# Signs, right combinations and row maxima of a two-layer graph kernel: a written order, another engine, and transposes

## The chip, the cores and the metric

The kernel runs on one core of a Trainium2 chip. The metric is the device time of one execution in microseconds; the time of a version is the median of its runs. An instruction belongs to an engine: TensorE (PE in the profile, its weight loads PEld), VectorE (DVE), ScalarE (ACT), GpSimd (POOL) or SyncE (SP, which here only issues transfers). Each engine works off its own queue in order and waits on semaphores for the others.

## The reference

`x` is 4096 x 512, `adj` 4096 x 4096 with non-negative entries, and all is float32. Two layers, each followed by a residual and a layer norm:

```python
# layer 0
xw  = maximum(sign(x), 0) @ sign(w0).T
x1  = layernorm(x + relu(adj @ xw))
# layer 1
node_att = softmax(x1 @ node_w, axis=0)
h   = x1 @ edge_w
e   = where(adj > 0, h @ h.T, NEG_BIG)
out = layernorm(x1 + (adj * (node_att * softmax(e, axis=1))) @ (x1 @ w1) + bias)
```

## The kernel before, in words

The 4096 rows are 32 blocks of 128, or 8 groups of 4 blocks (512 rows). The kernel goes through five stages, each bound to what the one before leaves in SBUF or in DRAM.

**Signs** (lines 167 to 256). `whole(g)` makes the four blocks of xw of a group g in two multiplications of 128 rows. Two blocks of signs are packed into one operand, `ba = [a > 0] + 2048 * [b > 0]` (lines 211 and 212, or 186 and 187 for group 0; the intermediate is `over0`). The weights' signs `bw` are made on VectorE in two passes a quarter (lines 204 and 206). The product `pw` is taken apart by a large shift: `us` on ScalarE (line 220), the low block on VectorE (222), the high one on ScalarE (223). In group 0 the four quarters of x and w0 arrive by separate transfers, and TensorE is kept active by multiplications of zeros (`zeros`).

Meanwhile the adjacency product of the first two row blocks (0 and 4, `early`) is accumulated. `halves(g)` loads two pieces `a`, rounds them to `hi` on ScalarE (line 236) and takes the remainder `lo` on VectorE (237); `follow(g)` multiplies both with xw, 16 matmuls a group (246 and 247). `hi`, `lo`, `over0` and `pos` come from one pool with two buffers a tag; `over0` has the tag of `hi`. `x` and w0 go through three buffers of `stream`, `a` through four of `rows`. A scheduler chooses the order on every engine here.

**Aggregation of layer 0** (345 to 384). For the other 30 blocks, `at` is split and multiplied in the same way (363 to 374, 64 matmuls a block); `rest` makes the layer norm and the products with `node_w`, and `transpose_rows` turns x1 into `x1T` with four transposes a block (333). `premask` loads pieces of adj, turns them into masks on VectorE (281) and stores them on GpSimd's queue (282). The order on VectorE and ScalarE is the written one.

**h** (387 to 429). `h.T` is made in four pairs of groups. Each pair is one step of a seven-product scheme: four combinations of the right operand, t1 to t4 (lines 417 to 420), t3 on GpSimd and the others on VectorE, and then `seven` (95 to 144), whose products go to three banks for each half q. A product that accumulates into a bank waits until VectorE or ScalarE has read what stood there. `between_h` is called between products and calls `premask` for three ticks of five. Tiles t1, t2 come from the tag of `hi`, t3, t4 from that of `lo`.

**e and its row maxima** (452 to 763): h @ h.T by blocks, with each block's negated row maximum in `nmax_c`.

**Aggregation of layer 1** (766 to 1420): 16 units `Aggregate(g, r)`, a written plan with due times as shares of a unit. Before the units of a group pair, `panel(A)` (777) spreads the maxima of 512 rows over all partitions: for each of its 4 blocks a multiplication takes the column of maxima, broadcast to 128 columns, as its stationary operand and the identity as the moving one (784). The result goes to `mrow` on ScalarE (795), which `shift` subtracts from e (835). There are eight panels, two before the units start and two ahead of each later group pair; the first pair stands in the stage of e. `Finish` ends rows with a product by w1 (1208) that VectorE adds to x1 (1219).

Of the kernel before, what the change touches and what calls it, by code (L numbers as in the profile page):

```python
# [22 lines left out]
TWO = 2.0**11  # L23
SHIFT = 1.5 * 2.0**34
SPLIT = 6, 4, 3
WARM = 12
# [3 lines left out]
def kernel(  # L30
# [128 lines left out]
    with (  # L159
# [14 lines left out]

        us = wp.tile([P, BG // 2, D], F32, name="us", tag="ends")

        def whole(g):

            xt = stream.tile([P, KD, W], F32, name="xt", tag="stream")
            ba = wp.tile([P, KD, W // 2], F32R, name="ba", tag="quarter", bufs=2)  # L180
            pws = [ps_mm.tile([P, D], F32, name="pw", tag="mm") for j in range(BG // 2)]
            order = [(k, j) for j in range(BG // 2) for k in range(KD)]

            def signs(k, over):
                a, b = xt[:, k, : W // 2], xt[:, k, W // 2 :]
                nc.vector.tensor_scalar(over, b, 0.0, TWO, ALU.is_gt, ALU.mult)
                nc.vector.scalar_tensor_tensor(ba[:, k, :], a, 0.0, over, ALU.is_gt, ALU.add)

            if g == 0:

                pos = sp.tile([P, KD, D], BF16, name="pos", tag="lo")
                over = sp.tile([P, KD, W // 2], F32, name="over0", tag="hi")
                for k in range(KD):
                    nc.sync.dma_start(w0[:, k, :], w0_t[ts(k, P), :])
                    nc.scalar.dma_start(xt[:, k, :], x_t[ts(k, P), ts(g, W)])
                idle = ps_mm.tile([P, D], F32, name="idle", tag="mm")

                def zeros(n):
                    for _ in range(n):
                        nc.tensor.matmul(idle, warm[:, :P], warm, start=True, stop=True)  # L200

                zeros(WARM)
                for k in range(KD):
                    nc.vector.tensor_scalar(pos[:, k, :], w0[:, k, :], 0.0, None, ALU.is_gt)
                    signs(k, over[:, k, :])
                    nc.vector.scalar_tensor_tensor(bw[:, k, :], w0[:, k, :], 0.0, pos[:, k, :], ALU.is_lt, ALU.subtract)
                order = [(k, j) for k in range(KD) for j in range(BG // 2)]
            else:
                nc.sync.dma_start(xt, x_t[:, ts(g, W)].rearrange("(k p) n -> p k n", p=P))
                over = sp.tile([P, KD, W // 2], F32, name="over0", tag="hi")  # L210
                nc.vector.tensor_scalar(over, xt[:, :, W // 2 :], 0.0, TWO, ALU.is_gt, ALU.mult)
                nc.vector.scalar_tensor_tensor(ba, xt[:, :, : W // 2], 0.0, over, ALU.is_gt, ALU.add)
            for k, j in order:
                nc.tensor.matmul(pws[j], ba[:, k, ts(j, P)], bw[:, k, :], start=(k == 0), stop=(k == KD - 1))  # L214
                if g == 0 and j == BG // 2 - 1:
                    zeros(3 if k < KD - 1 else 5)
                if k == KD - 1:

                    u = us[:, j, :]
                    nc.scalar.activation(u, pws[j], AF.Identity, bias=shift[:, 0:1])  # L220
                    b = g * BG + j
                    nc.vector.scalar_tensor_tensor(xw[:, b, :], u, SHIFT, pws[j], ALU.subtract, ALU.subtract)
                    nc.scalar.activation(xw[:, b + BG // 2, :], u, AF.Identity, bias=shift[:, 1:2], scale=-1.0 / TWO)


        early = [0, BG]
        accs = []

        def halves(g):

            hi = sp.tile([P, QC, P], F32R, name="hi", tag="hi")
            lo = sp.tile([P, QC, P], F32R, name="lo", tag="lo")
            for n, b in enumerate(early):
                a = rows.tile([P, BG, P], F32, name="a0", tag="rows")
                nc.sync.dma_start(a, adj_t[b, :, ts(g, BG), :])
                nc.scalar.copy(hi[:, ts(n, BG), :], a)
                nc.vector.tensor_sub(lo[:, ts(n, BG), :], a, hi[:, ts(n, BG), :].bitcast(F32))
            return hi, lo

        def follow(g, hi, lo):  # L240
            if g == 0:
                accs.extend(ps_tr.tile([P, D], F32, name="acc0", tag="tr") for _ in early)
            for n in range(2):
                for c in range(BG):
                    kb = g * BG + c
                    nc.tensor.matmul(accs[n], hi[:, n * BG + c, :], xw[:, kb, :], start=(kb == 0), stop=False)  # L246
                    nc.tensor.matmul(accs[n], lo[:, n * BG + c, :], xw[:, kb, :], start=False, stop=(kb == NB - 1))  # L247

        whole(0)
        parts = halves(0)  # L250
        for g in range(NG):
            if g + 1 < NG:
                whole(g + 1)
            follow(g, *parts)
            if g + 1 < NG:
                parts = halves(g + 1)

        nw_b = wp.tile([P, D], F32, name="nw_b")
        nc.sync.dma_start(nw_b, bass.AP(tensor=node_w.tensor, offset=node_w.offset, ap=[[0, P], [1, D]]))
# [31 lines left out]
        def rest(n, b, xb, acc, before):  # L291

            mv = small.tile([P, 1, nc.vector.BN_AGGR_DIM], F32, name="mv")
            stats = small.tile([P, nc.vector.BN_STATS_DIM], F32, name="stats")
            rstd = small.tile([P, 1], F32, name="rstd")
            scr = wp.tile([P, D], F32, name="scr")
            nc.vector.scalar_tensor_tensor(xb, acc, 0.0, xb, ALU.max, ALU.add)
            nc.vector.bn_stats(stats, xb)
            nc.vector.bn_aggr(mv[:, 0, :], stats)
            yield  # L300
            nc.scalar.activation(rstd, mv[:, :, 1], AF.Sqrt, bias=eps)
            nc.vector.reciprocal(rstd, rstd)
            nc.vector.tensor_scalar(xb, xb, mv[:, 0, 0:1], rstd[:, 0:1], ALU.subtract, ALU.mult)
            nc.vector.tensor_tensor_reduce(
                scr, xb, nw_b, 1.0, 0.0, ALU.mult, ALU.add, accum_out=node_s[:, b : b + 1]
            )
            yield
            nc.vector.tensor_add(scr, xb, bias_b)
# [28 lines left out]
        parts = deque()  # L337
# [65 lines left out]
        for _ in range(4):  # L403
            premask(nc.sync, 0, 3)
        count = [0]

        def between_h(q, n):
            count[0] += q is None
            if q is None and count[0] > 6 and count[0] % 5 % 2 == 0:
                premask(nc.sync, 0, 3)  # L410

        for g in range(HG):
            r11, r12 = (x1T[:, :HK, ts(c, W)] for c in (g, g + HG))
            r21, r22 = (x1T[:, HK:, ts(c, W)] for c in (g, g + HG))
            t1, t2 = (sp.tile([P, HK, W], F32, name="t12", tag="hi") for _ in range(2))
            t3, t4 = (sp.tile([P, HK, W], F32, name="t34", tag="lo") for _ in range(2))
            nc.vector.tensor_sub(t1, r12, r11)
            nc.gpsimd.tensor_sub(t3, r22, r12)
            nc.vector.tensor_sub(t2, r22, t1)
            nc.vector.tensor_sub(t4, r21, t2)  # L420
            right_h = r11, r21, r22, t4, t1, t2, t3
            seven(
                lambda m, q: [left_h[m][:, k, ts(q, P)] for k in range(HK)],
                lambda m: [right_h[m][:, k, :] for k in range(HK)],
                [[hT[:, q + f, ts(c, W)] for f in (0, HK) for c in (g, g + HG)] for q in range(2)],
                between_h,
            )
# [349 lines left out]
    def panel(A):  # L777
# [4 lines left out]
        for i in range(BG):  # L782

            nc.tensor.matmul(
                pt[:, ts(i, P)],
                nm[:, i : i + 1].to_broadcast([P, P]),
                ident,
                start=(i == 0),
                stop=True,
                skip_group_check=i > 0,  # L790
            )
        if A > 1:
# [664 lines left out]
```

## Time and profile before

| | |
|---|---|
| median of 5 runs | 1937.34 us (1936.02 to 1939.8) |
| the profiled execution | 1939.8 us, its span 1937.8 us |
| granted TensorE clock, mean | 0.998 |
| first matmul of the aggregation of layer 0 (line 373) | at 57.13 us |
| first product of h, first product of e | at 507.44 and 605.80 us |
| first product of the aggregation of layer 1 | at 1091.94 us |
| busy of the engines from 507 to 606 us | PE 97.9, DVE 67.6, ACT 12.4, POOL 32.5 us |
| data moved | 508.72 MB, mean 263 GB/s |

A span runs from the first to the last instruction. A row of the timeline has start, duration, engine, line, operation, output and inputs, and at its end, in brackets, how long the engine had been idle and what released it. The ends of matmuls are modelled: one of 512 columns is shown with 0.39 us (fp32r) though the next starts 0.23 us after it, so starts are compared, not durations. Some rows that the steps below use, each as mean duration:

| line | engine | what | us |
|---|---|---|---|
| 204, 206 | DVE | bw, a quarter | 0.42, 0.68 |
| 186, 187 | DVE | over0 and ba of group 0, a quarter | 0.29, 0.42 |
| 211, 212 | DVE | over0 and ba, a whole group | 0.69, 1.23 |
| 220, 223 | ACT | us, high block of xw | 0.69, 0.72 |
| 222 | DVE | low block of xw | 0.69 |
| 236, 237 | ACT, DVE | hi, lo | 0.62, 0.69 |
| 417, 419, 420 | DVE | t1, t2, t4 | 1.22 to 1.23, one 3.27 |
| 418 | POOL | t3 | 2.36 to 3.20 |

Independent neighbours on an engine overlap by some 0.1 us of these.

### The profile page before, as it was taken

Reading aid. Unit: us, or ns where it says so; the run is one execution under the profiler, and the core shown is the slowest. Engines: PE = TensorE matmul, PEld = TensorE weight load, DVE = VectorE, ACT = ScalarE, POOL = GpSimd, SP = SyncE. Lnnn points to the kernel's source line nnn. Section 1 sums busy time; section 2 is a strip of 40 time slices with the busy share of each in tenths; the row PEclk is TensorE's granted clock in tenths of the full one; section 3 lists DMA queues with packets and bytes.
Section 4 is the critical chain, followed back from the end, with each engine's and each line's share of the span. In section 5 each row is a group of like instructions: output and inputs, shape, how many; then the busy total and the mean of one; then the engine's idle time right before and its main releaser. Section 6 shows DMA issues by size and latency. Waiting matters only on the chain.

```text
span 1937.8 us, 20238 instructions
## 1 busy us (share of the span) xinstructions
PE 1919.1 (99%) x6742; PEld 1204.2 (62%) x6742; DVE 1389.7 (72%) x2062; ACT 1022.4 (53%) x1614; POOL 292.2 (15%) x413
## 2 busy tenths in 40 slices
PE   9999999999999999999999999999999999999998
PEld 6888888888644445454556444456666666666655
DVE  7766676676765566567665986687869987798747
ACT  5433333333202567566677666546766576757731
POOL 0122222222341111011111111111111110111100
PEclk9999999999999999999999999999999999999999
DMA  8888888888475478577783998787778777877731
GB/s 308 299 326 309 293 324 306 326 305 291 152 274 214 165 254 318 184 280 252 278 314 105 347 328 290 264 273 257 260 265 291 261 272 260 293 274 262 274 109 44
DMA packets 169527, 508.72 MB, mean 263 GB/s; under 512 B 15696, under 2 KB 41040, under 8 KB 161744
## 3 DMA queue, kind: packets, MB, share of 16 engines
q1 hardware_dynamic: 89472, 226.39, 35.1%
q0 software_dynamic: 64688, 239.10, 32.9%
q10 hardware_dynamic: 15264, 41.95, 5.9%
q8 instruction: 53, 0.87, 0.2%
q14 instruction: 50, 0.41, 0.1%
HBM read 385.74 MB, written 121.63 MB: 262 GB/s over the span
## 4 chain that ended last, share of the span: by engine, by line
PE 88%; issue 4%; DMA 4%; DVE 3%; ACT 1%; POOL 1%; POOLq 0%; DVEq 0%; SPq 0%
PE bank L1081 32%; PE seven L714 15%; PE acc L374 11%; PE acc L373 11%; PE pe L641 6%; PE po L1208 3%; PE seven L101 3%; PE pt L603 3%; DMA slot<-s_d 1%; DMA lent<-s_d 1%; PE pw L214 1%; PE acc L246 1%; PE pt L333 1%; PE acc L247 1%; DMA over<-in_w_dram 1%
## 5 line engine op out<-in xcount | busy, mean ns | idle before, releaser
L1081 PE MATMUL bank<-lent,lop 128*128 128x512 f32 (+1 forms) x1136 | 420.0, 517 | 0.0
L373 PE MATMUL acc<-xw,hi 128*128 128x512 f32 x960 | 376.4, 392 | 0.0
L374 PE MATMUL acc<-xw,lo 128*128 128x512 f32 x960 | 374.2, 390 | 0.0
L1081 PE MATMUL bank<-slot,lop 128*128 128x256 f32 (+1 forms) x1052 | 357.8, 488 | 1.9 <-DVE slot L862 1.9
L1081 PEld LDWEIGHTS bank<-lent,lop 128*128 128x128 f32 x1136 | 215.7, 190 | 173.9 <-issue 158.8
L1081 PEld LDWEIGHTS bank<-slot,lop 128*128 128x128 f32 x1052 | 200.2, 191 | 136.7 <-issue 116.4
L363 ACT CAST hi<-at 128x1024 fp32r<-128x1024 f32 x120 | 126.4, 1054 | 203.4 <-PE acc L373 148.4
L365 DVE TENSOR_TENSOR lo<-at,hi 128x1024 fp32r<-128x1024 f32 x120 | 148.0, 1234 | 84.7 <-ACT hi L363 84.7
L374 PEld LDWEIGHTS acc<-xw,lo 128*128 128x128 f32 x960 | 180.3, 188 | 37.0 <-DVE lo L365 0.3
L373 PEld LDWEIGHTS acc<-xw,hi 128*128 128x128 f32 x960 | 180.3, 188 | 36.7
L1090 ACT COPY over<-bank 128x512 f32<-128x512 f32 x200 | 114.3, 580 | 108.3 <-PE bank L1081 95.3
L641 PE MATMUL pe<-hT 128*128 128x512 f32 (+3 forms) x384 | 132.1, 486 | 0.0
L574 ACT ACTIVATE line<-line,nmax_c 128x512 f32<-128x512 f32 x160 | 114.8, 725 | 22.5 <-DVE nmax_c L565 22.3
L565 DVE CUSTOM_DVE_ANT_0 line<-lent,slot 128x512 f32<-128x512 bf16 x140 | 90.7, 688 | 48.4 <-ACT slot L651 26.7
L835 DVE CUSTOM_DVE_ANT_1 lent<-lent,line 128x2048 f32<-128x2048 f32 x40 | 91.4, 2286 | 27.4 <-DMA lent<-s_d 17.2
L838 ACT ACTIVATE lent<-lent 128x2048 f32<-128x2048 f32 x40 | 76.5, 1912 | 58.3 <-DVE lent L835 58.3
L841 ACT ACTIVATE slot<-slot 128x2048 f32<-128x2048 f32 x36 | 68.8, 1912 | 66.4 <-DMA slot<-in_adj_t_dram 59.7
L641 PEld LDWEIGHTS pe<-hT 128*128 128x128 f32 x384 | 64.6, 191 | 41.4 <-issue 33.8
L714 PE MATMUL seven<-hT 128*128 128x512 f32 x192 | 89.8, 593 | 0.0
L1053 ACT COPY bank<-over 128x512 f32<-128x512 f32 x144 | 84.9, 596 | 3.0 <-DVE left L973 0.2
L603 PEld LDWEIGHTS pt<-ident,lent 128*128 128x128 f32 x418 | 52.2, 141 | 52.1 <-issue 38.8
L604 ACT COPY slot<-pt 128x512 f32<-128x512 f32 (+3 forms) x123 | 68.4, 559 | 24.0 <-PE pt L603 24.0
(262 smaller groups left out, 2849.9 us busy)
## 6 DMA issues: line engine op xcount, KB each, us to landing
at<-in_adj_t_dram SPq DMA_DIRECT2D x60, 1024.0 KB, 6.7
lop<-lop_d SPq DMA_DIRECT2D x79, 512.0 KB, 4.6
lent<-s_d POOLq DMA_DIRECT2D x39, 1024.0 KB, 7.7
slot<-in_adj_t_dram POOLq DMA_DIRECT2D x38, 1024.0 KB, 7.2
s_d<-slot POOLq DMA_DIRECT2D x30, 1024.0 KB, 7.4
lent<-in_adj_t_dram POOLq DMA_DIRECT2D x26, 1024.0 KB, 7.4
lop<-lop_d SPq DMA_DIRECT2D x99, 256.0 KB, 4.2
lent<-in_adj_dram SPq DMA_DIRECT2D x48, 512.0 KB, 5.7
```

The lines of the kernel that those rows point to most:

```text
L363: nc.scalar.copy(hi, aq)
L365: nc.vector.tensor_sub(lo, aq, hi.bitcast(F32))
L373: nc.tensor.matmul(acc, hi[:, c, :], xw[:, kb, :], start=(kb == 0), stop=False)
L374: nc.tensor.matmul(acc, lo[:, c, :], xw[:, kb, :], start=False, stop=(kb == NB - 1))
L565: nc.vector.tensor_tensor_reduce(line, mask, src, -1.0, HUGE, ALU.add, ALU.min, accum_out=nmax_c[:, b, c : c + 1])
L574: nc.scalar.activation(line, line, AF.Exp, bias=nmax_c[:, b, c : c + 1], scale=-1.0, accum_out=sum_c[:, b, c : c + 1])
L603: nc.tensor.transpose(pt[:, j, :], src[:, ts(j, P)], ident)
L641: nc.tensor.matmul(pe[:, lo * P :], hT[:, k, ts(A * BG + i, P)], hT[:, k, (B * BG + lo) * P : (B + 1) * W], start=(k == 0), stop=(k == KD ...
L714: nc.tensor.matmul(ps, left[m][:, k, q, :], right[m][:, k, :], start=(first and k == 0), stop=(k == KD // 2 - 1), skip_group_check=not first,)
L835: pinned[0](nc.vector._custom_dve(TENSOR_ADD_SAT, out=q, in0=q, in1=m, s0=0.0, s1=-HUGE))
L1081: nc.tensor.matmul(ps, lop[:, k, :], rop[:, k, :], start=start, stop=(k == K - 1), skip_group_check=True)
L1090: nc.scalar.copy(self.to(), self.bank[:, : self.w])
```

## The change

Four things are changed. The signs of w0 are made on ScalarE in one pass a quarter, by the Sign function, whose table is loaded while the data are under way. The sign stage is written out in order for VectorE, ScalarE and TensorE; x is loaded two groups ahead, its signs are made up to two groups ahead, `over0` gets a buffer of its own (bfloat16, under the tag of `scr`), and `follow` is divided into its two blocks, with `whole` of the next group between them. In h the combinations of a pair are made during the pair before, and t3 is made on VectorE. The multiplications of `panel` get `is_transpose=True`.

```diff
-                for k in range(KD):
-                    nc.vector.tensor_scalar(pos[:, k, :], w0[:, k, :], 0.0, None, ALU.is_gt)
-                    signs(k, over[:, k, :])
-                    nc.vector.scalar_tensor_tensor(bw[:, k, :], w0[:, k, :], 0.0, pos[:, k, :], ALU.is_lt, ALU.subtract)
...
+            over = wp.tile([P, KD, W // 2], BF16, name="over0", tag="scr")
...
+            for k in range(KD):
+                nc.scalar.activation(bw[:, k, :], w0[:, k, :], AF.Sign, scale=-1.0)
+                a, b = (xt[:, k, h] for h in halves)
+                nc.vector.tensor_scalar(over[:, k, :], b, 0.0, TWO, ALU.is_gt, ALU.mult)
+                nc.vector.scalar_tensor_tensor(ba[:, k, :], a, 0.0, over[:, k, :], ALU.is_gt, ALU.add)
...
+        with tc.manual_schedule(
+            engines={mybir.EngineType.DVE, mybir.EngineType.Activation, mybir.EngineType.PE}
+        ):
...
+            for n in range(2):
+                load_a(0, n)
+            load_x(1)
+            signs_x(0)
+            whole(0, 0)
+            split(0, 0)
+            whole(0, 1)
+            split(0, 1)
+            signs_x(1)
+            for g in range(NG):
+                follow(g, 0)
+                if not g:
+                    follow(g, 1)
+                if g + 1 < NG:
+                    for n in range(2):
+                        load_a(g + 1, n)
+                    if g + 2 < NG:
+                        load_x(g + 2)
+                    split(g + 1, 0)
+                    if g:
+                        split(g + 1, 1)
+                        if g + 2 < NG:
+                            signs_x(g + 2)
+                    for j in range(2):
+                        whole(g + 1, j)
+                    if not g:
+                        signs_x(g + 2)
+                        split(g + 1, 1)
+                if g:
+                    follow(g, 1)
...
+        def rights_h(g):
...
             nc.vector.tensor_sub(t1, r12, r11)
-            nc.gpsimd.tensor_sub(t3, r22, r12)
             nc.vector.tensor_sub(t2, r22, t1)
+            yield
+            t3, t4 = (sp.tile([P, HK, W], F32, name="t34", tag="lo") for _ in range(2))
+            nc.vector.tensor_sub(t3, r22, r12)
+            yield
             nc.vector.tensor_sub(t4, r21, t2)
+            rights[g] = r11, r21, r22, t4, t1, t2, t3
+            yield
...
+        def between_h(q, n):
+            count[0] += q is None
+            if q is None and count[0] % 14 in (8, 10, 13) and ahead_h:
+                next(ahead_h.popleft())
...
@@ panel
                 start=(i == 0),
                 stop=True,
+                is_transpose=True,
                 skip_group_check=i > 0,
```

In the new order `split(g, n)` makes hi and lo of one block of a group, `follow(g, n)` makes its eight matmuls (in the order 0, 2, 1, 3 of the columns), `whole(g, j)` one packed product with its three readers, and `signs_x(g)` over0 and ba of a group.

More of the change, by code (lines that the diff above doesn't have):

```diff
@@ L175 @@
         us = wp.tile([P, BG // 2, D], F32, name="us", tag="ends")
-        def whole(g):
-            xt = stream.tile([P, KD, W], F32, name="xt", tag="stream")
-            ba = wp.tile([P, KD, W // 2], F32R, name="ba", tag="quarter", bufs=2)
[L181 to L192, printed above, removed]
-                for k in range(KD):
[L194 to L203, printed above, removed]
-                    nc.vector.tensor_scalar(pos[:, k, :], w0[:, k, :], 0.0, None, ALU.is_gt)
-                    signs(k, over[:, k, :])
-                    nc.vector.scalar_tensor_tensor(bw[:, k, :], w0[:, k, :], 0.0, pos[:, k, :], ALU.is_lt, ALU.subtract)
[L207 to L223, printed above, removed]
@@ L226 @@
[L226 to L238, printed above, removed]
@@ L240, in follow @@
-        def follow(g, hi, lo):
-            if g == 0:
-                accs.extend(ps_tr.tile([P, D], F32, name="acc0", tag="tr") for _ in early)
-            for n in range(2):
[L244 to L256, printed above, removed]
+        early = [0, BG]
+        accs, xts, rights_s, split_a = [], {}, {}, {}
+        halves = [slice(h * (W // 2), (h + 1) * (W // 2)) for h in range(2)]
+        def load_x(g):
+            xts[g] = stream.tile([P, KD, W], F32, name="xt", tag="stream")
+            if g:
+                nc.sync.dma_start(xts[g], x_t[:, ts(g, W)].rearrange("(k p) n -> p k n", p=P))
@@ new lines, in load_a, with signs_x @@
+        def load_a(g, n):
+            a = rows.tile([P, BG, P], F32, name="a0", tag="rows")
+            nc.sync.dma_start(a, adj_t[early[n], :, ts(g, BG), :])
+            split_a[g, n] = a
+        def signs_x(g):
+            xt = xts.pop(g)
+            ba = wp.tile([P, KD, W // 2], F32R, name="ba", tag="quarter", bufs=2)
+            over = wp.tile([P, KD, W // 2], BF16, name="over0", tag="scr")
+            rights_s[g] = ba
+            if g:
+                nc.vector.tensor_scalar(over, xt[:, :, halves[1]], 0.0, TWO, ALU.is_gt, ALU.mult)
+                nc.vector.scalar_tensor_tensor(ba, xt[:, :, halves[0]], 0.0, over, ALU.is_gt, ALU.add)
+                return
+            for k in range(KD):
[3 more added lines that the diff above has]
+                nc.vector.scalar_tensor_tensor(ba[:, k, :], a, 0.0, over[:, k, :], ALU.is_gt, ALU.add)
@@ new lines, in zeros, with whole @@
+        def zeros(n):
+            for _ in range(n):
+                nc.tensor.matmul(idle, warm[:, :P], warm, start=True, stop=True)
+        def whole(g, j):
+            pw = ps_mm.tile([P, D], F32, name="pw", tag="mm")
+            for k in range(KD):
+                nc.tensor.matmul(pw, rights_s[g][:, k, ts(j, P)], bw[:, k, :], start=(k == 0), stop=(k == KD - 1))
+                if g == 0 and (not j or k == KD - 1):
+                    zeros(2 if not j else 4)
+            u = us[:, j, :]
+            nc.scalar.activation(u, pw, AF.Identity, bias=shift[:, 0:1])
+            b = g * BG + j
+            nc.vector.scalar_tensor_tensor(xw[:, b, :], u, SHIFT, pw, ALU.subtract, ALU.subtract)
+            nc.scalar.activation(xw[:, b + BG // 2, :], u, AF.Identity, bias=shift[:, 1:2], scale=-1.0 / TWO)
@@ new lines, in split, with follow @@
+        def split(g, n):
+            if not n:
+                hi = sp.tile([P, QC, P], F32R, name="hi", tag="hi")
+                lo = sp.tile([P, QC, P], F32R, name="lo", tag="lo")
+                split_a[g] = hi, lo
+            (hi, lo), a = split_a[g], split_a.pop((g, n))
+            nc.scalar.copy(hi[:, ts(n, BG), :], a)
+            nc.vector.tensor_sub(lo[:, ts(n, BG), :], a, hi[:, ts(n, BG), :].bitcast(F32))
+        def follow(g, n):
+            hi, lo = split_a[g]
+            for c in (0, 2, 1, 3):
+                kb = g * BG + c
+                nc.tensor.matmul(accs[n], hi[:, n * BG + c, :], xw[:, kb, :], start=(kb == 0), stop=False)
+                nc.tensor.matmul(accs[n], lo[:, n * BG + c, :], xw[:, kb, :], start=False, stop=(kb == NB - 1))
@@ new lines @@
+        with tc.manual_schedule(
+            engines={mybir.EngineType.DVE, mybir.EngineType.Activation, mybir.EngineType.PE}
+        ):
+            load_x(0)
+            for k in range(KD):
+                nc.sync.dma_start(w0[:, k, :], w0_t[ts(k, P), :])
+                nc.scalar.dma_start(xts[0][:, k, :], x_t[ts(k, P), :W])
+            nc.scalar.activation(us[:, 0, 0:1], eps, AF.Sign)
+            idle = ps_mm.tile([P, D], F32, name="idle", tag="mm")
+            accs.extend(ps_tr.tile([P, D], F32, name="acc0", tag="tr") for _ in early)
+            zeros(WARM)
+            for n in range(2):
+                load_a(0, n)
[16 more added lines that the diff above has]
+                    split(g + 1, 0)
+                    if g:
+                        split(g + 1, 1)
[6 more added lines that the diff above has]
+                        split(g + 1, 1)
+                if g:
+                    follow(g, 1)
@@ L295, in rest @@
             rstd = small.tile([P, 1], F32, name="rstd")
-            scr = wp.tile([P, D], F32, name="scr")
+            scr = wp.tile([P, D], F32, name="scr", tag="scr")
             nc.vector.scalar_tensor_tensor(xb, acc, 0.0, xb, ALU.max, ALU.add)
@@ L405 @@
         count = [0]
+        rights = {}
+        def rights_h(g):
+            r11, r12 = (x1T[:, :HK, ts(c, W)] for c in (g, g + HG))
+            r21, r22 = (x1T[:, HK:, ts(c, W)] for c in (g, g + HG))
+            t1, t2 = (sp.tile([P, HK, W], F32, name="t12", tag="hi") for _ in range(2))
+            nc.vector.tensor_sub(t1, r12, r11)
+            nc.vector.tensor_sub(t2, r22, t1)
+            yield
+            t3, t4 = (sp.tile([P, HK, W], F32, name="t34", tag="lo") for _ in range(2))
+            nc.vector.tensor_sub(t3, r22, r12)
+            yield
+            nc.vector.tensor_sub(t4, r21, t2)
+            rights[g] = r11, r21, r22, t4, t1, t2, t3
+            yield
+        ahead_h = deque(p for g in range(1, HG) for p in [rights_h(g)] * 3)
+        for _ in rights_h(0):
+            pass
         def between_h(q, n):
             count[0] += q is None
+            if q is None and count[0] % 14 in (8, 10, 13) and ahead_h:
+                next(ahead_h.popleft())
             if q is None and count[0] > 6 and count[0] % 5 % 2 == 0:
@@ L412 @@
         for g in range(HG):
[L413 to L421, printed above, removed]
+            right_h = rights.pop(g)
             seven(
```

## The prediction

> **What bounds the kernel now.** I read the page first, then TensorE's own waits, then the three places that the change touches in the timeline.
>
> ```profile
> span 1937.8 us, 20238 instructions
> PE 1919.1 (99%) x6742; PEld 1204.2 (62%) x6742; DVE 1389.7 (72%) x2062; ACT 1022.4 (53%) x1614; POOL 292.2 (15%) x413
> ```
>
> TensorE is busy for 99% of the span and its granted clock is 0.998. So a microsecond counts only if it comes off TensorE's own work or off one of its few waits. All of those, from the wait table limited to TensorE (engine and line that waited, releaser, total us, times, longest):
>
> ```profile
> PE po L1208 <- DVE xb L1219: 5.3, 6, 1.4
> PE bank L1081 <- DVE slot L862: 1.9, 1, 1.9
> PE acc L246 <- DVE xw L222: 1.3, 4, 0.6
> PE idle L200 <- DVE warm L168: 1.3, 1, 1.3
> PE seven L101 <- DVE hT L122: 1.0, 1, 1.0
> ```
>
> Only two rows lie in the changed stages: L246 (signs) and L101 (h), 2.3 us together. Anything more must come from TensorE work that disappears, or from waits that this view cannot show because TensorE filled them with warming matmuls.
>
> **Panels: the row maxima as transposes.** The timeline of TensorE around one pair of panels, and the last transposes of x1 before the h stage (start, duration, what, count):
>
> ```profile
> 1441.07 1.95 PE L784 MATMUL bank<-ident,nm 128*128 128x128 f32 x16
> 1442.85 1.45 PE L1081 MATMUL bank<-lent,lop 128*128 128x512 f32 x3
> ...
> 507.01 0.60 PE L333 MATMUL pt<-ident,xb 128*128 128x128 f32 x4
> 507.44 1.02 PE L101 MATMUL seven<-x1T,we_s 128*128 128x512 f32 x2
> ```
>
> The sixteen records are eight multiplications: 8 panels x 4 columns are 32 calls, and the line has 64 records, two for each. They hold TensorE from 1441.07 to 1442.85, 1.78 us, or 0.89 for a panel. Line 333 has 128 records for 32 blocks x 4 calls, one each, and its four take 507.01 to 507.44, 0.43 us. A panel as four transposes thus saves 0.89 - 0.43 = 0.46, and eight save 3.7 us. The first two panels stand at 1029.18 to 1030.07 and at 1042.20, in the e stage; TensorE has no gap there either, so I count them.
>
> [...] I take -3.7, with -3.7 and +1.7 as the ends.
>
> **h: right combinations ahead, all on VectorE.** The third pair's stall:
>
> ```profile
> 570.49 2.36 POOL L418 TENSOR_TENSOR t<-x1T 128x1024 f32<-128x1024 f32 x1
> 570.67 3.27 DVE L419 TENSOR_TENSOR t<-x1T,t 128x1024 f32<-128x1024 f32 x1
> 573.86 0.67 DVE L122 TENSOR_TENSOR hT<-hT,seven 128x512 f32<-128x512 f32 x1
> 574.59 0.70 PE L101 MATMUL seven<-t,we_s 128*128 128x512 f32 x1 [1.01 <-DVE hT L122]
> ```
>
> L419 takes 1.22 to 1.23 us elsewhere; beside GpSimd's subtraction it took 3.27, and L122, queued behind it, came too late for the bank that TensorE wanted at 573.58. The change adds four 1.22 us subtractions to VectorE (4.9 us) and removes four on GpSimd (2.4 to 3.2 us each). VectorE is busy 67.6 of the 99 us between 507 and 606, so the 4.9 us fit into its idle time. The order of the instructions puts t1 and t2 ahead of L122 and t3 between two L122/L123 pairs. L122's bank is wanted 3.43 us after its product ends, and 1.2 us of t3 fits. GpSimd's queue then has only mask stores, so a load of `more` that waited for such a store (its mask op idled VectorE 4.06 us until 568.74) comes sooner or at the same time. One new wait: 1/gsum on VectorE now stands between two L131, where GpSimd's reduction may come late; L131's bank is wanted only by the next pair, 6 us later. If the cover were gone, each 1.22 us ahead of L122 would come back as stall. I take -1.0, with -1.2 (the stall and the slower first matmul behind it) and +1.0.
>
> **Signs.** Sixteen `follow` and eight `whole` matmuls a group at 0.2265 us (the spacing of starts) are 5.44 us. Before, `whole` starts at 15.71, 21.24, 27.13, 32.92, 38.82, 44.61, 50.51 in the chain of work that ended last: 5.8 a group, 7 x 0.36 = 2.5 us above the work. What a group waits for:
>
> ```profile
> 25.57 1.23 DVE L212 SCALAR_TENSOR_TENSOR ba<-xt,over 128x1024 fp32r<-128x1024 f32 x1
> 26.88 0.62 ACT L236 CAST hi<-a 128x512 fp32r<-128x512 f32 x1 [1.91 <-DVE ba L212]
> 26.96 0.40 PE L214 MATMUL pw<-bw,ba 128*128 128x512 f32 x1
> ...
> 57.13 0.39 PE L373 MATMUL acc<-xw,hi 128*128 128x512 f32 x1
> ```
>
> `over0` sits in the buffers of `hi`, so ScalarE's cast waits for L212. The change gives it its own buffer, and in the steady state everything then precedes need: VectorE has 0.61+0.61+0.73+1.14+0.6+0.6, some 4.6 us by its spacings, ScalarE about 4, TensorE 5.44.
>
> But the new order must be reached, so I walk the queues by the measured spacings. The last quarter of x lands at 8.77 (issue at 2.2 and 6.6 to landing), its signs end at 9.54, and the last k starts at 9.6 instead of 10.69: the four VectorE passes for bw (0.42 + 0.68 each) had been the limit; four Signs on ScalarE (0.6, as a cast or an activation of that size) lie beside the landings. That is 1.1 won. Then one pair at a time: ScalarE runs us 10.14, xw 10.86, cast 11.49, us 12.0, xw 12.7, cast 13.4 to 14.0. VectorE's lo follows at 14.03, over and ba for group 1 at 14.64 and 15.37, ba's end 16.6. TensorE ends follow(0) at 16.4 and starts whole(1) at 16.65. `us` needs 1.17 after that, so xw of its second pair ends at 20.55, and over, ba (group 2), lo, lo, lo, over, ba (group 3) come before xw of group 2 in the written order: ba(2) ends 22.4, xw 26.75. TensorE waits about 0.8 and 0.4 in follow(1), 1.0 ahead of whole(2), 0.6 in follow(2), and whole(3) starts at 28.6. From there nothing is late, and 128 matmuls x 0.2265 = 29.0 end the stage at 57.6, against 57.13 before: +0.5. What was won at 9.6 and in the period is thus spent on filling the two-group lead. The ends: +1.8 if each handover costs 0.1 us more than I walked; and, with no such waits, 16.4 + 168 x 0.2265 = 54.5, which is -2.6.
>
> SP's queue: `a` of group 2 waits for lo at 12.8 and 14.7 (it was issued at 11.26), and x(3) stands behind it, issued at about 15.1 instead of 12.26. The queues of data are full until then (98% busy from 15 to 30 us), so x(3) still lands near 21.4, ahead of 24.2 where VectorE takes it.
>
> **The rest.** A scheduler places the later stages, and its order on VectorE and ScalarE shifts a little around the panels (a reduction, an exponential of 0.23 us, a combination up or down by one or two places; TensorE's order is the same). The nearest row is L1208's six waits of 0.5 to 1.4: one more or one fewer. I take 0, ends -1 and +1.5.
>
> Sum: -3.7 - 1.0 + 0.5 + 0 = -4.2 us. The profiled execution took 1939.8 (span 1937.8 and 2.0 around it), so it would take 1935.6; from the median, 1937.34, I get 1933.1.
>
> **Rivals.**
> (a) The walk is too slow and the sign stage pays: its -2.6 instead of +0.5 gives -7.3, 1930.0. For it: the period of 5.8 is visibly a buffer wait, which goes. Against: VectorE's written order puts 6 us of other work before xw of group 2.
> [...]
> (c) Slower: x arrives late. Every x(g+2) now stands on SP behind `a` that waits for a lo, and VectorE takes it in a fixed place, ahead of xw. In the steady state it is issued at about 29.1 (x(6)) and taken at 39.8, 10.7 us; landing took 7.4 in the median and 9.1 at most. Beyond 10.7, each microsecond passes to TensorE in five groups. To end slower by 0.2% it has to eat 4.2 and 3.9 more, so 12.3 us to landing: 1941.5.
>
> **How the numbers follow.** A measurement of this kernel can tell 0.2%, 3.9 us, from no change. My forecast, 0.54 (its own range -5.7 to -2.7), lies astride that bound: 0.35 faster, 0.19 same. Rival (a) 0.24, faster. Rival (b) 0.15, same. Rival (c) 0.07: slower 0.06, same 0.01. Together 0.59 faster, 0.35 same, 0.06 slower. The range runs from just above (a)'s end, 1930.3, to 1936.2, which takes in my forecast's slow side and half of (b).
>
> **What would show it.** Right: panel records 32 instead of 64, four in 0.43 us; no wait of L101 on L122, and t2 at 1.22 us; the sign stage's last matmul near 57.6 with whole(1) at 16.7 and whole(3) at 28.6 and a 5.44 us period after that. Wrong: waits of TensorE on ba or xw beyond group 3, new waits of L1208 or L1081 on VectorE behind the panels, or transposes further apart than 0.11 us.

## The result, and the profile after

The changed kernel takes 1932.58 us (median of 25 runs, 1929.87 to 1936.74) against 1936.62 for the kernel before in runs beside it (45 runs, 1934.33 to 1942.14): a ratio of 0.9978 with an interval of 0.9973 to 0.9983, 4.0 us faster. The forecast was 1933.1 us. Measured again later, unchanged (e7 below), the ratio was 0.9975 [0.9966, 0.9984].

The profiled execution took 1933.57 us, with a span of 1931.8 (before 1937.8). First the busy times and TensorE's waits of the kernel after; the lines are counted anew, so that the product by w1, line 1208 before, is now 1244, and h's product is still line 101.

```profile
span 1931.8 us, 20169 instructions
PE 1912.1 (99%) x6708; PEld 1200.1 (62%) x6708; DVE 1387.2 (72%) x2058; ACT 1024.1 (53%) x1619; POOL 279.4 (14%) x409
```

```profile
PE po L1244 <- DVE xb L1255: 4.9, 5, 1.4
PE pw L213 <- DVE ba L204: 1.9, 3, 1.4
PE bank L1117 <- DVE slot L898: 1.6, 1, 1.6
...
PE acc L235 <- DVE xw L219: 1.0, 2, 0.6
PE pw L213 <- DVE ba L198: 0.7, 1, 0.7
```

The row of L101 on L122 is gone, and two rows of the sign stage, on `ba`, are new (1.9 and 0.7 us). A pair of panels, then the third pair of h, in the timeline of the kernel after:

```profile
1436.86 1.04 PE L819 MATMUL bank<-ident,nm 128*128 128x128 f32 x8
1437.73 2.74 PE L1117 MATMUL bank<-lent,lop 128*128 128x512 f32 x6
```

```profile
566.77 1.22 DVE L434 TENSOR_TENSOR t<-x1T 128x1024 f32<-128x1024 f32 x1
568.32 1.23 DVE L435 TENSOR_TENSOR t<-x1T,t 128x1024 f32<-128x1024 f32 x1 [0.34 <-PE seven L101]
...
570.07 0.68 DVE L122 TENSOR_TENSOR hT<-hT,seven 128x512 f32<-128x512 f32 x1
```

The pair of panels holds TensorE for 0.87 us instead of 1.78, with 8 records instead of 16. In h, t2 (L435) takes 1.23 instead of 3.27, and L122 begins 61.06 us behind h's first product instead of 66.42. From starts on TensorE, the 6.0 us between the two executions lie here. The last two rows meet at the product that waits for `slot` (1091.94 and 1090.88 us); the table of before calls it the first of layer 1's aggregation, but 32 products of that line stand ahead of it, from 1076.18 and 1075.35 us.

| stretch, by TensorE's starts | before | after | difference |
|---|---|---|---|
| to the first product of layer 0's aggregation | 57.13 | 58.68 | +1.55 |
| from there to h | 450.31 | 450.33 | 0.0 |
| h | 98.36 | 96.88 | -1.48 |
| e, with two panels and those 32 products | 486.14 | 484.99 | -1.15 |
| from there to the start of TensorE's last four products | 838.14 | 833.18 | -4.96 |

The fourth row holds two panels (-0.91) and the wait for `slot` (1.86 and 1.63, so -0.23). The last row holds six panels (5.36 and 2.63, so -2.73), waits of the product by w1 (5.27 and 4.92, -0.35), and 1.7 us that only this execution has: behind its wait of 1.86 us the granted clock was 0.91 from 1090 to 1110 us, and the distance from the product behind the wait to the next panel was 135.70 instead of 134.00. All the other executions profiled for this study have 134.00 or 134.01 there, with either form of h and of the signs.

### The profile page after: what moved, and what is told of

Read it like the earlier page. It is cut to its first block, busy times and chain, and to the rows that moved or that the text cites. A ratio compares the mean times of both kernels' runs of the same rounds, so it can differ in the third digit from the quotient of the medians.

```text
span 1931.8 us, 20169 instructions
## 1 busy us (share of the span) xinstructions
PE 1912.1 (99%) x6708; PEld 1200.1 (62%) x6708; DVE 1387.2 (72%) x2058; ACT 1024.1 (53%) x1619; POOL 279.4 (14%) x409
## 4 chain that ended last, share of the span: by engine, by line
PE 85%; DVE 6%; DMA 4%; issue 3%; ACT 2%; POOL 0%; ACTq 0%; DVEq 0%; POOLq 0%
PE bank L1117 29%; PE seven L749 14%; PE acc L396 11%; PE acc L395 11%; PE pe L676 6%; PE seven L101 5%; PE po L1244 3%; PE pt L638 2%; DMA slot<-s_d 1%; DMA slot<-in_adj_t_dram 1%; PE pt L355 1%; DVE lent L883 1%; PE acc L236 1%; PE acc L235 1%; PE pw L213 1%
```

## The experiments

The first three have one part of the change alone. A difference in us is between means of runs on the same chip; where a bound is given, it is twice the error of the difference of the two means.

**Panels alone (e1).** The kernel before with only

```diff
                 stop=True,
+                is_transpose=True,
                 skip_group_check=i > 0,
```

> The kernel before with nothing but the panels' multiplications turned into transposes. My theory (each panel holds TensorE 0.46 us less, nothing else late): -3.7 us, ratio about 0.9981, nearly the whole gain; panel records 32, a pair of panels from its first start to the next product 0.87 to 0.9 us instead of 1.78, no new waits behind them. Rival (the gain comes from the h and sign stages, the panels only move the wait): -1 us or less, ratio 0.9995 or more, with new waits of L1208 or L1081 on VectorE. [...]

Measured: 1933.18 us, ratio 0.9973 [0.9964, 0.9982], as much as the whole change. The difference of the means, 5.4 +- 1.1 us, is more than TensorE's own work saved: four pairs of panels at 0.91 are 3.65. All the panels' records in e1, with minimum, median and maximum duration in ns:

```profile
L784 PE MATMUL bank<-ident,nm x24: 272/273/273, 1223.3 to 1645.4; 128*128 128x128 f32 x24
...
L784 PE MATMUL ptm<-ident,nm x8: 272/272/273, 1027.9 to 1040.8; 128*128 128x128 f32 x8
```

Each shows 272 to 273 ns, but eight of them hold TensorE for 0.87 us, 0.109 a record: the 272 ns are a latency.

**h alone (e2).** The kernel before with the new h:

```diff
-            nc.gpsimd.tensor_sub(t3, r22, r12)
+            nc.vector.tensor_sub(t3, r22, r12)
...
+            if q is None and count[0] % 14 in (8, 10, 13) and ahead_h:
+                next(ahead_h.popleft())
```

> The kernel before with nothing but the new h stage. Theory: the one stall of L101 on L122 goes, with the slower products behind it; from the first product of h to the first of e 96.9 us instead of 98.4, so -1.0 to -1.5 us, ratio 0.9992 to 0.9995. Rival (the stall belongs to that one profiled execution and others have none): ratio 1.000 though the profile is 1.5 us shorter there.

Measured: 1937.73 us, ratio 1.0001 [0.9992, 1.001]. In its profile h takes 96.87 us and has no wait. The gain of h is thus not seen in the time of this kernel alone; the interval would let up to 1.6 us through.

**Signs alone (e3).** The kernel before with the new sign stage (the first half of the diff above):

```diff
+                nc.scalar.activation(bw[:, k, :], w0[:, k, :], AF.Sign, scale=-1.0)
...
+        with tc.manual_schedule(
```

> The kernel before with nothing but the new sign stage. Theory (the work to get two groups ahead eats what the earlier start and the steady period win): first matmul of the aggregation at 57.6 to 58.7 us against 57.1, ratio 1.0002 to 1.0008, waits of TensorE on ba and xw up to group 2 and none later. Rival (the stage gains): first matmul at 55 to 56 us, ratio 0.9990 to 0.9995.

Measured: 1938.67 us, ratio 1.0003 [0.9993, 1.0012]. The stage ended at 58.03 in its profile, within the 57.6 to 58.7 that were expected, and h, in its old form here, took 98.62.

**Signs one group ahead (e4).** The kernel after, its sign stage in another written order: a group's signs stand between the two `whole` of the group ahead, and both `follow` are divided in the same way in every group. The signs of group 1, too, come earlier, ahead of the second `split` of group 0. `over_x` and `ba_x` are the two operations of `signs_x`.

```diff
...
-                    if g:
-                        split(g + 1, 1)
-                        if g + 2 < NG:
-                            signs_x(g + 2)
-                    for j in range(2):
-                        whole(g + 1, j)
...
+                    split(g + 1, 1)
+                    whole(g + 1, 0)
+                    if g + 2 < NG:
+                        over_x(g + 2)
+                    whole(g + 1, 1)
+                    if g + 2 < NG:
+                        ba_x(g + 2)
+                follow(g, 1)
```

> The changed kernel with its sign stage in another written order: signs of group 1 ahead of the second lo of group 0, follow of block 1 always behind whole of the next group, and the signs of group g+2 behind and between the xw of group g+1 (over0 between the two, ba after the second) and not two groups ahead. Same instructions. Theory (only the order of VectorE's queue in the first three groups costs): no wait on ba or xw from group 2 on, first matmul of the aggregation at 55.3 to 56.4 us, 2 to 2.5 us ahead of the changed kernel; ratio to before 0.9966 to 0.9969. Rival (data or PE are late anyway in the first 20 us): it ends within 0.5 us of the changed kernel's 57.6 to 58.7, ratio 0.9978.

Measured: 1929.7 us (five runs), ratio 0.9961 [0.995, 0.9973]: faster than both kernels. The last quarter's first product and the first `whole` of groups 1 and 2 on TensorE in e4, then the same of the kernel after:

```profile
10.15 0.47 PE L224 MATMUL pw<-bw,ba 128*128 128x512 f32 x1
...
15.86 2.11 PE L224 MATMUL pw<-bw,ba 128*128 128x512 f32 x8 [0.58 <-DVE ba L215]
...
21.44 1.98 PE L224 MATMUL pw<-bw,ba 128*128 128x512 f32 x8
...
55.89 0.39 PE L402 MATMUL acc<-xw,hi 128*128 128x512 f32 x1
```

```profile
10.44 0.47 PE L213 MATMUL pw<-bw,ba 128*128 128x512 f32 x1 [0.16 <-DVE ba L204]
...
17.38 2.14 PE L213 MATMUL pw<-bw,ba 128*128 128x512 f32 x8
20.10 0.50 PE L235 MATMUL acc<-xw,hi 128*128 128x512 f32 x1 [0.58 <-DVE xw L219]
...
23.36 2.11 PE L213 MATMUL pw<-bw,ba 128*128 128x512 f32 x8 [0.74 <-DVE ba L198]
...
27.70 0.50 PE L235 MATMUL acc<-xw,hi 128*128 128x512 f32 x1 [0.42 <-DVE xw L219]
29.66 1.99 PE L213 MATMUL pw<-bw,ba 128*128 128x512 f32 x8
```

From the last quarter (10.15 in e4, 10.44 after) to the stage's end e4 needs 45.74 us and the kernel after 48.24. These 2.5 us are the price of the order with a lead of two groups; with a lead of one nothing waits from group 2 on. As e4 moves the signs of group 1 and `follow` of group 0 as well, it does not show what the lead alone costs. By the means beside the kernel before, e4 is 8.65 +- 1.4 us faster and the kernel after 4.3 +- 0.8; whether more than the stage's 2.5 us lies between them these bounds do not tell.

**What is the surplus of e1?** The cheaper panels also moved instructions. In the aggregation of layer 1 the kernels e2 and e3 have VectorE and ScalarE in the order of the kernel before, instruction by instruction; e1 and e4 have that of the kernel after (at least 44 of VectorE's last 900 instructions have to be moved to make one order into the other), and TensorE's order is the same in all. Work theory: only TensorE's own time counts. Order theory: this order is worth something itself. Kernels whose panels cost a little more tell them apart, because the scheduler goes back to nearly the old order between six and seven transposes a panel, and between two and one of four (e5 is 10 and e12 is 7 such moves from the kernel before; e6 and e11 are 3 from the kernel after).

```diff
@@ e5: one of four as a transpose; e6: i < 2
-                is_transpose=True,
+                is_transpose=i < 1,
@@ e11: six transposes a panel; e12: range(3), seven
-        for i in range(BG):
+        for i in [*range(BG), *range(2)]:
```

> The kernel after, with one of a panel's four multiplications as a transpose instead of four, so that a panel costs TensorE about 0.11 + 3 x 0.22 = 0.77 us (before 0.89, after 0.44). The scheduler's order on VectorE and ScalarE is then nearly that of the kernel before. Work theory (only TensorE's own time of the panels counts): 8 x 0.33 = 2.7 us more than the kernel after, ratio to before about 0.9992. Order theory (the order that came with the cheap panels is worth 2 to 3 us of waits in the aggregation of layer 1): 2.7 + 2.5 us more than the kernel after, ratio about 1.0005, and 837 us or more from the first product of that aggregation to TensorE's last start, with the products by w1 waiting 5 us or more.

> The kernel after, with two of a panel's four multiplications as transposes: 2 x 0.11 + 2 x 0.22 = 0.66 us a panel, 0.9 us for eight less than with one of four. The scheduler's order is then nearly that of the kernel after. Work theory: 0.9 us faster than with one of four. Order theory: 0.9 + 2.5 = 3.4 us faster than with one of four, 832 to 835 us from the first product of the aggregation of layer 1 to TensorE's last start, with the products by w1 waiting 3 to 5 us.

> The kernel after, unchanged, beside the two others on the same chip. Work theory: 1.8 us faster than two of four and 2.7 faster than one of four. Order theory: 1.8 and 5.2 faster. Ratio to before 0.9975 to 0.9982 either way. In its profile the 6 panels behind the first product of the aggregation of layer 1 take 0.44 us each.

> The kernel after, with six transposes a panel instead of four (two columns are made twice): 6 x 0.107 = 0.64 us a panel. The scheduler's order is nearly that of the kernel after. Work theory and order theory alike: 8 x 0.21 = 1.7 us more than the kernel after, ratio to before about 0.9986 to 0.9989.

> The kernel after, with seven transposes a panel: 0.75 us. The scheduler's order is nearly that of the kernel before. Work theory: 8 x 0.107 = 0.9 us more than with six. Order theory, with the size that the runs with one and two of four gave it: 0.9 + 1.7 = 2.6 us more than with six (mean of the runs, as the medians of eleven runs move by 0.5).

Measured (e5 to e7 shared a chip, and e11 and e12; the work is four times the difference in what a pair of panels holds TensorE by the profiles: 0.87 us in e7, 1.33 in e6, 1.56 in e5, 1.31 in e11, 1.53 in e12):

| kernel | order | us | ratio to before | compared | slower by, us | work of it, us |
|---|---|---|---|---|---|---|
| e7, after again | new | 1932.24 | 0.9975 [0.9966, 0.9984] | | | |
| e6, two of four | near new | 1934.84 | 0.9989 [0.998, 0.9998] | with e7 | 2.5 +- 1.1 | 1.8 |
| e5, one of four | near old | 1937.13 | 0.9999 [0.9991, 1.0008] | with e7 | 4.7 +- 1.1 | 2.7 |
| | | | | with e6 | 2.2 +- 1.1 | 0.9 |
| e11, six | near new | 1934.56 | 0.9983 [0.9974, 0.9991] | | | |
| e12, seven | near old | 1936.51 | 0.9996 [0.9987, 1.0005] | with e11 | 2.1 +- 1.3 | 0.9 |

The two steps over the border cost 1.3 and 1.2 us more than the work, e5 against e7 2.0 more, and e1 against before 1.75 more (5.4 - 3.65). Each alone is at the edge of what the runs resolve; all four point the same way, though e5 serves in two of them. So TensorE's own time is not all that counts. The order theory fits, with about 1 to 2 us instead of the 2.5 that was expected of e5 and e6, but it is not shown. A rival without any order fits within the bounds too: each microsecond of panels would cost about 1.5 us of time, which makes 2.7 of e6 against e7, 1.4 of e5 against e6, 1.3 of e12 against e11 and 5.5 of e1. Against it stands only that the two smaller steps, which cross the border, cost more than that (2.2 and 2.1), and the larger one that does not cross it cost less (2.5).

Where these microseconds lie the profiles show only in part. A forecast on it missed: e5 was to take 837 us or more from the wait for `slot` to TensorE's last products, with 5 us or more of waits by the product by w1, and its profiled execution took 833.14 with 2.5. This product waits for VectorE at nearly the same places in all kernels, and the sum changes from one execution to the next: 5.3, 7.2, 7.9, 3.1, 2.5, 4.9 us in the order of before or near it, 4.9, 3.0, 3.1, 5.1, 4.6, 6.1, 4.7, 4.7 in that of after or near it, which are means of 5.2 and 4.5. What comes in the old order alone, but for one case in e6, is a wait of 0.8 to 1.4 us between 1730 and 1771 us (in four of six executions). Its chain in the kernel before:

```profile
1764.60 2.29 DVE L835 CUSTOM_DVE_ANT_1 slot<-slot,line 128x2048 f32<-128x2048 f32 x1 [3.43 <-DMA slot<-s_d]
1766.81 0.48 DVE L1219 SCALAR_TENSOR_TENSOR xb<-po,f,xb 128x256 f32<-128x256 f32 x1
...
1767.34 1.13 PE L1208 MATMUL po<-line,line 128*128 128x256 f32 x4 [0.87 <-DVE xb L1219]
```

and the same place in the kernel after:

```profile
1758.52 2.29 DVE L871 CUSTOM_DVE_ANT_1 slot<-slot,line 128x2048 f32<-128x2048 f32 x1 [3.08 <-DMA slot<-s_d]
1760.57 1.03 PE L1244 MATMUL po<-over 128*128 128x256 f32 x4
1760.73 0.48 DVE L1255 SCALAR_TENSOR_TENSOR xb<-po,f,xb 128x256 f32<-128x256 f32 x1
...
1761.43 1.03 PE L1244 MATMUL po<-line,line 128*128 128x256 f32 x4
```

VectorE has idled for 3 us until `slot` lands, and the sum into xb, which frees TensorE's bank, stands behind the operation on `slot`. TensorE's products ahead of the wait start 0.84 us after VectorE's start on `slot` in the kernel before (1765.44 - 1764.60) and 2.05 us after it in the kernel after (1760.57 - 1758.52): the load came 1.2 us earlier against TensorE's work, and the wait of 0.87 is gone. So in these two executions the wait comes from a landing. Whether and how a different order of VectorE and ScalarE brings the load forward stays open, and so does the order of before with cheap panels, which no run has.

**Which part of the new h counts (e8, e9).** e8 is the kernel after with t3 back on GpSimd, still ahead; e9 is the kernel before with t3 on VectorE, not ahead.

```diff
@@ e8, on the kernel after
-            nc.vector.tensor_sub(t3, r22, r12)
+            nc.gpsimd.tensor_sub(t3, r22, r12)
@@ e9, on the kernel before
-            nc.gpsimd.tensor_sub(t3, r22, r12)
+            nc.vector.tensor_sub(t3, r22, r12)
```

> The kernel after, with t3 of h back on GpSimd, still made during the pair before. Exclusion theory (a tensor operation of GpSimd and one of VectorE of these kinds never run together: the later one waits until the earlier has ended): VectorE operations that start under a t3 show up to 2.2 us more, t3 itself 2.36 us where it comes first and up to 3.2 where it comes second; as t3 is two steps behind t1 and t2, these two stay at 1.22, TensorE has at most 0.3 us of waits, and h takes 96.9 to 97.3 us. Rival (any GpSimd work in h costs TensorE a stall, wherever it stands): 98 us or more, with a wait of a product of h on VectorE of about 1 us.

> The kernel before, with t3 of h on VectorE and nothing ahead. Exclusion theory: the third pair's t2 takes 1.22 us in any execution, there is no wait of a product of h on VectorE's combination, and h takes 96.9 us: being ahead adds nothing. Rival (what counts is being ahead; the third pair's combinations come late behind a mask that waits for its load): t1 starts near 569 after h started at 507, and a wait of 0.5 to 1.3 us stays, h 97.5 to 98.4 us.

Measured: h takes 101.84 us in e8 and 96.88 in e9. (Single runs: 1938.47 and 1935.28 us, beside 1938.39 for the kernel before.) In e8, t3 of the third pair and then the third pair itself, during which t3 of the fourth is made:

```profile
560.53 2.34 POOL L438 TENSOR_TENSOR t<-x1T 128x1024 f32<-128x1024 f32 x1 [10.64 <-issue]
562.83 1.65 POOL L304 DMA_DIRECT2D mask_d<-more  x2
...
573.72 0.69 DVE L303 TENSOR_SCALAR more<-more 128x1024 bf16<-128x1024 f32 x1 [5.01 <-DMA more<-in_adj_dram]
574.33 0.68 DVE L122 TENSOR_TENSOR hT<-hT,seven 128x512 f32<-128x512 f32 x1
575.06 1.98 PE L101 MATMUL seven<-t,we_s 128*128 128x512 f32 x4 [0.75 <-DVE hT L122]
575.46 2.35 POOL L438 TENSOR_TENSOR t<-x1T 128x1024 f32<-128x1024 f32 x1
575.65 2.72 DVE L303 TENSOR_SCALAR more<-more 128x1024 bf16<-128x1024 f32 x1
...
579.02 3.48 PE L101 MATMUL seven<-t,we_s 128*128 128x512 f32 x4 [1.98 <-DVE hT L122]
```

Two things go wrong. GpSimd's t3 stands in its queue until 560.53, and the mask stores behind it come late; `more` lands late, and VectorE's mask idles for 5.01 us with L122 behind it (0.75 us of TensorE). And the next mask, 0.69 us long elsewhere, begins 0.19 us behind t3 and takes 2.72 (1.98 us of TensorE). The first was in no theory on record: the expectation of at most 97.3 failed, and the rival's 98 us or more came true for a reason that it did not name. In e9 the third pair's t2, an L122 and t3 stand so:

```profile
567.77 1.22 DVE L419 TENSOR_TENSOR t<-x1T,t 128x1024 f32<-128x1024 f32 x1 [0.34 <-PE seven L101]
...
571.42 0.68 DVE L122 TENSOR_TENSOR hT<-hT,seven 128x512 f32<-128x512 f32 x1
572.02 1.22 DVE L418 TENSOR_TENSOR t<-x1T 128x1024 f32<-128x1024 f32 x1
```

Each takes its usual time and no product of h waits, so being ahead is not needed.

**Signs of w0 on VectorE in the new order (e10).** The kernel after, with a buffer for `pos`, without the early load of Sign's table, and with

```diff
-                nc.scalar.activation(bw[:, k, :], w0[:, k, :], AF.Sign, scale=-1.0)
+                nc.vector.tensor_scalar(pos[:, k, :], w0[:, k, :], 0.0, None, ALU.is_gt)
+                nc.vector.scalar_tensor_tensor(bw[:, k, :], w0[:, k, :], 0.0, pos[:, k, :], ALU.is_lt, ALU.subtract)
```

> The kernel after, with the weights' signs made on VectorE in two passes a quarter, as before, in the new order. Theory (the four passes for bw were the limit of the first quarters): the last quarter's product starts at 10.7 to 11.5 instead of 10.4 us, and the first product of the aggregation of layer 0 about as much later, 59.0 to 59.8. Rival (the landing of x is the limit in most executions): within 0.2 us of the landing plus 0.9 us, as in the kernel after, and the stage ends at 58.5 to 58.9.

Measured (a single run, 1935.39 us beside 1938.39 for the kernel before): the stage ends at 60.43, against 57.85 to 58.71 in the eight profiles that have the sign stage of the kernel after unaltered. TensorE on the first quarters in e10:

```profile
8.24 0.51 PE L215 MATMUL pw<-bw,ba 128*128 128x512 f32 x1 [0.45 <-DVE ba L206]
...
9.97 0.50 PE L215 MATMUL pw<-bw,ba 128*128 128x512 f32 x1 [0.77 <-DVE ba L206]
...
11.69 0.51 PE L215 MATMUL pw<-bw,ba 128*128 128x512 f32 x1 [0.78 <-DVE ba L206]
```

A quarter comes every 1.72 us, near the 1.81 of the four passes in the table (0.29 + 0.42 + 0.42 + 0.68), and the last starts 1.25 us later than in the kernel after. The theory was right in kind; the cost at the stage's end, 2.0 us against the mean of 58.4, put the end beyond the 59.8 expected at most. Where the 0.75 us beyond the 1.25 lie is not shown.

## Why the prediction was right, step by step

**Panels, -3.7: right in size and mechanism.** 8 x 0.456 = 3.65 in the pairs' own times, 0.107 us a transpose, and no fall of the clock: the mean granted clock is 1.000 in the kernel after and 0.999 in e1. The panels' other end, +1.7, and with it the 0.15 of rival (b), no run shows: each call is one record here, of 272 to 273 ns, and eight of them hold TensorE for 0.87 us.

**The rest, 0 with -1 and +1.5: mis-sized.** "The nearest row is L1208's six waits of 0.5 to 1.4: one more or one fewer. I take 0". Four comparisons show 1 to 2 us beyond the panels' own work, with the changed order on VectorE and ScalarE as the likely but unproven cause. Whether they lie in the row that was named is not shown (means of 5.2 and 4.5). What the prediction did not ask is that the row is a sample of one execution: in others of the same or nearly the same order it was 2.5 to 7.9.

**h, -1.0: right in the profile, not confirmed in time.** h went from 98.36 to 96.88. But the stall is no fixed property of the kernel before: with the old h it stood in two of three profiled executions (98.36, 98.62 in e3, 96.87 in e1), while with t3 on VectorE h took 96.87 or 96.88 in every one. In e1 GpSimd's t3 began 0.48 us behind VectorE's t2 instead of 0.18 us ahead of it. In the term "four 1.22 us subtractions" and the freed queue of GpSimd the working was right (e8 shows the queue's part, 0.75 us of TensorE); "ahead" added nothing (e9). What the prediction called slow "beside GpSimd's subtraction" is exclusion, and is told below. The time of e2 shows 0.65 +- 1.3 us of gain.

**Signs, +0.5: right in mechanism, a little small.** The stage ended at 57.13, 57.31, 58.03 and 58.15 in the four profiles with its old form, mean 57.66, and at 58.4 in the mean of eight with the new one: +0.7. Step by step in the kernel after: the last quarter at 10.44, not 9.6, as x landed 0.77 later in that execution; whole(1) 6.94 us behind it (walked 7.05), whole(3) 12.28 behind that (walked 11.95), the period 5.44 from then on, and waits of 0.58, 0.74 and 0.42 where 0.8 and 0.4, 1.0 and 0.6 were walked. "What was won [...] is thus spent on filling the two-group lead" agrees with e4: in an order without that lead 2.5 us stay. The bound of the walk without waits was 54.5; e4 ended at 55.89. Rival (a), with -2.6, named this place rightly, but is the result of e4, not of this change. Rival (c) did not happen: no product waits for `ba` behind group 2.

The sum of -4.2 against -4.0 measured (-4.3 and -4.8 by the means of the two sets of runs) owes something to luck: -3.65 for the panels, +0.7 for the signs, -1 to -2 for what came with the panels, and h between 0 and -1.5 make -4 to -6.5.

## What to carry to other kernels

Where a scheduler places the rest, a cheaper instruction can also change the order: compare orders between the builds, and test kernels that lie on either side of the change of order, before a surplus is put down to the instruction. A wait seen in one profile can be a draw (h in its old form took 98.36, 98.62 and 96.87 us in three); ask what decides the race (here who starts first, or when a load lands), and look at several executions before it is booked as a saving. And signs made further ahead cost their place in the queue at the start: in the profile of e4, with a lead of one group instead of two, the same operations ended 2.5 us sooner.

## What the runs showed of the hardware

**VectorE and GpSimd excluded each other here.** In the pairs below, an operation with its operands in SBUF that started while the other engine's subtraction ran ended when a full turn of its own had followed the other's end, less about 0.13 us. The two orders, in e3 (GpSimd first) and in e1 (VectorE first):

```profile
571.66 2.36 POOL L440 TENSOR_TENSOR t<-x1T 128x1024 f32<-128x1024 f32 x1
571.85 3.26 DVE L441 TENSOR_TENSOR t<-x1T,t 128x1024 f32<-128x1024 f32 x1
```

```profile
570.02 1.22 DVE L419 TENSOR_TENSOR t<-x1T,t 128x1024 f32<-128x1024 f32 x1
570.50 2.96 POOL L418 TENSOR_TENSOR t<-x1T 128x1024 f32<-128x1024 f32 x1 [0.69 <-PE seven L101]
571.16 0.68 DVE L122 TENSOR_TENSOR hT<-hT,seven 128x512 f32<-128x512 f32 x1
...
572.48 1.53 DVE L281 TENSOR_SCALAR more<-more 128x1024 bf16<-128x1024 f32 x1
```

In e3, GpSimd's remaining 2.17 and VectorE's 1.22 are 3.39, shown 3.26. In e1, VectorE's remaining 0.74 and GpSimd's 2.36 are 3.10, shown 2.96; the mask of L281 pays the remaining 0.98 and 0.69 (1.67, shown 1.53). The mask of e8 above pays 2.16 and 0.69 (2.85, shown 2.72), and the 3.27 of before is 2.18 + 1.22 - 0.13. L122, which reads `seven` in PSUM, runs at its usual 0.68 under t3 in e1. What makes the engines exclude each other these runs do not show. A lead of 0.2 us on GpSimd's side (before, e3) or of 0.5 on VectorE's (e1) decided whether TensorE lost 1.0 and 1.3 us or nothing.

**The clock behind short waits.** In e8 the granted clock of the stretch behind the waits of 0.75 and 1.98 us fell:

```profile
570.00:575.00 5.00, 4.31 (x11) 1.56 (x9) 1.28 (x2) 1.17 (x2) 0.29 (x1) 1.00 0.99 399
575.00:585.00 10.00, 7.96 (x14) 3.27 (x15) 8.28 (x11) 0.00 (x0) 4.96 (x5) 0.83 0.89 311
585.00:600.00 15.00, 15.00 (x36) 6.65 (x35) 9.22 (x15) 1.17 (x2) 2.90 (x4) 1.00 0.35 128
```

The third number from the end is the granted clock, 0.83 in the second row and 1.00 in the rows around it: 0.17 of 10 us, or 1.7 us. By TensorE's starts, the four products from 579.02 us took 3.27 us instead of 1.72, and the eight behind them 3.68 instead of 3.43. With the 2.7 us of waits these 1.7 are most of the 4.96 us by which h was longer. In the kernel before it is 0.51 from 1092.2 to 1095.7 us, behind the wait of 1.86 us: the 0.91 of 1090 to 1110 us, and the 1.7 us lost there. In e4, with one wait of 1.70 us between 1086 and 1106 us, it stayed at 1.00 over this stretch, and so it did in e7 from 1534 to 1556 us, where TensorE stood still for 1.86 us in all. So the wait of the kernel before cost nearly twice its length (1.86 and 1.7 us), and that of e4 only its own 1.70; what decides is not settled here.
